# Graph product of the first layer as seven block products, with the block sums made in place by VectorE and GpSimd

## The chip, the cores and the metric

The kernel runs on one core of one Trainium2 chip. The metric is the device time of one execution in microseconds (us); lower is better. Before the change the median of three timed runs is 2531.78 us (2531.7 to 2536.01).

The engines are called as the profile calls them: PE is TensorE, DVE is VectorE, ACT is ScalarE, POOL is GpSimd, and SP is SyncE, which only issues transfers. SBUF is the on-chip memory that all of them read, PSUM the accumulators that PE writes. Each engine works through its own instructions strictly in order, and semaphores hold an instruction back until its inputs, or the buffer that it overwrites, are free.

## The reference

Two layers work on x (16 batches of 1024 rows and 256 columns, fp32) and share a 1024 x 1024 matrix `adj`. The change is in the first layer:

```python
fea = jnp.transpose(x, (0, 2, 1))                       # 256 x 1024 a batch
c_adj = jnp.mean(fea, axis=1)
diff = c_adj[:, None, :] - c_adj[:, :, None]
A = jnp.abs(jnp.abs(jax.nn.sigmoid(diff) - 0.5) - 0.5) * 2.0
Wg = adj[None, :, :] * (A + jnp.transpose(A, (0, 2, 1))) * 0.5
g = jnp.einsum('bcn,bnm->bcm', fea, Wg)                 # the graph product
q = relu(g * para)                                      # queries of 4 heads
k, v = x @ kv_w                                         # keys and values
out = softmax(q k^T * scale) v
x = layernorm(x + out)
```

For every batch the graph product multiplies 256 x 1024 by 1024 x 1024, and its result, weighted with `para` and rectified, are the queries of an attention over 1024 keys with 4 heads. The second layer (a product with a normalised `adj`, two linear maps with batch norms, a layer norm) is untouched by the change.

## The kernel before

`fast_path` does the first layer batch by batch under a manual schedule: PE, ACT, DVE and SP execute in the order in which the program is written, and POOL in an order that the framework chooses.

The attention of a batch is 32 units (2 pairs of heads x 2 halves of 512 queries x 8 blocks of 128 keys), taken two at a time: 16 bursts, u = 0 to 15. In burst u PE first makes the scores of its two units (`scores`, L952, into `ps`), ACT takes the exponential (L957, into `p`), and then `back(u-1)` multiplies the burst before with the values (`outputs`, L973, into `po`). DVE adds up the exponentials for the denominators (L981 for the first two units of a half, L983 for the others). `p` has four buffers, so an exponential needs the DVE sum of the unit four places earlier. `ps`, 128 x 1024 fp32 and two PSUM banks wide, has two buffers, and the accumulators `pg` of the graph product come from the same two. At the end of a half (u = 4, 8, 12 and 0) ACT copies `po` (L990), DVE adds to it (L991) and transposes it (L1001).

Between the bursts of batch b the written order places the preparation of batch b+1 and b+2 and the end of batch b-1:

- u = 0: values and keys of batch b+1 on PE (L902, L889), and part of its graph weights `wg`, eight tiles of 128 x 1024: ACT takes |difference| (`weights_abs`, L833) and a tanh (`weights_tanh`, L838), DVE multiplies with `adj` (`weights_adj`, L842). `side` is the list of these 24 steps, run two or three at a time.
- u = 1 and 11: `residual` of a pair of heads on POOL (L1047, L1048), after DVE reciprocals (L1041).
- u = 4: layer norm of batch b-1. `statistics_x1` is 8 pairs of DVE instructions (L620, L621), a chain of four small POOL instructions (L593, L595, L625, L626) that ends in `nm_l`, and `finish_x1` is 8 ACT instructions (L630) that need `nm_l`; then POOL issues the store of x (L1069). On PE stand here the graph product of batch b+1 for columns 0 to 127 (`graph_mm`, c = 0) and the last keys.
- u = 5: SP issues the load of x for batch b+2 and of its first half in squares of 32 x 32 (`load_squares`, L762, into `xS`, one buffer).
- u = 8: `begin` for batch b+2 on DVE (a row sum, L788, and the column means `ccol` and `ncol`, L790 and L794), a store and a broadcast load of the means by SP (L795, L797, into `crow`), the first `transpose_squares` on DVE (L813); on PE the graph product for columns 128 to 255 (c = 1) and the denominators (`normalise`, L1020).
- u = 9 to 15: first part of the weights of batch b+2; at u = 11 the second `transpose_squares`.

One half of the columns takes 16 matmuls of 128 x 128 by 128 x 512, eight in each bank of `pg`; the profile counts every fp32 matmul as two records. When all 16 are done, `queries` weights them on DVE (L861) and rectifies them on ACT (L864). Batch 0's product stands apart (`graph_first`, L874).

```python
for hs in (H0, H1):
    nc.tensor.matmul(
        s["pg"][:, hs], xt[:, n, c * P : (c + 1) * P], s["wg", n][:, hs],
        start=(n == 0), stop=(n == NCH - 1),
    )
if n == NCH - 1:
    queries(c, slice(0, N), s["pg"])
```

Of the kernel before, what the change touches and what calls it, by code (L numbers as in the profile page):

```python
# [10 lines left out]
F32 = mybir.dt.float32  # L11
I32 = mybir.dt.int32
AF = mybir.ActivationFunctionType
ALU = mybir.AluOpType
# [4 lines left out]
P = 128  # L19
# [496 lines left out]
def fast_path(  # L516
# [43 lines left out]
    def tile_s(name):  # L560
        return psum["s"].tile([P, N], F32, tag="s", name=name)
# [48 lines left out]
    def layernorm_steps(t, name):  # L610


        st = small.tile([P, NCH, 6], F32, tag="ln_st", name=f"st_{name}")
        mv = small.tile([P, NCH, 2], F32, tag="ln_mv", name=f"mv_{name}")
        rstd = small.tile([P, NCH], F32, tag="ln_rs", name=f"rs_{name}")
        nmr = small.tile([P, NCH], F32, tag="ccol", name=f"nm_{name}")

        def statistics(ns=range(NCH)):
            for n in ns:
                nc.vector.bn_stats(st[:, n, :], t[:, n, :])  # L620
                nc.vector.bn_aggr(mv[:, n, :], st[:, n, :])  # L621
            if NCH - 1 not in ns:
                return
            rsqrt(rstd, mv[:, :, 1], EPS)
            nc.gpsimd.tensor_tensor(nmr, mv[:, :, 0], rstd, ALU.mult)  # L625
            nc.gpsimd.tensor_scalar(nmr, nmr, -1.0, None, ALU.mult)  # L626

        def apply(ns=range(NCH)):
            for n in ns:
                nc.scalar.activation(  # L630
                    t[:, n, :], t[:, n, :], AF.Identity,
                    bias=nmr[:, n : n + 1], scale=rstd[:, n : n + 1],
                )

        return statistics, apply
# [68 lines left out]
    H0, H1 = slice(0, HALF), slice(HALF, N)  # L704
    C0, C1 = slice(0, P), slice(P, C)
    M0, M1 = slice(0, NCH // 2), slice(NCH // 2, NCH)
# [18 lines left out]
    graph = ExitStack()  # L725
# [7 lines left out]
    with (  # L733
# [40 lines left out]
        def prologue(b):  # L774


            s = st[b]
            xt = s["x"]
            first, steps, side = [], [], []

            def step(f, *a):
                steps.append((f, a))
# [27 lines left out]
            def transpose_squares(c):  # L810
                if c == 0:
                    s["xT"] = xTp.tile([P, CC, N], F32, tag="xT", name=f"xT_{b}")
                nc.vector.transpose(  # L813
                    s["xT"][:, c, :], s["xS", c].rearrange("p j i -> p (j i)")
                )
                if c == 0:
                    load_squares(b, 1)

            def row_of_means():

# [22 lines left out]
                    w, w, 1.0, adj_s[:, n, :], op0=ALU.subtract, op1=ALU.mult  # L843
                )

            def graph_mm(c, n):
                if n == 0:
                    s["pg"] = tile_s(f"pg_{b}_{c}")
                    if c == 0:
                        s["qT"] = qkv.tile([P, CC, N], F32, tag="qT", name=f"qT_{b}")  # L850
                for hs in (H0, H1):
                    nc.tensor.matmul(  # L852
                        s["pg"][:, hs], xt[:, n, c * P : (c + 1) * P], s["wg", n][:, hs],
                        start=(n == 0), stop=(n == NCH - 1),
                    )
                if n == NCH - 1:
                    queries(c, slice(0, N), s["pg"])

            def queries(c, hs, ps):
                q = s["qT"][:, c, hs]  # L860
                nc.vector.scalar_tensor_tensor(  # L861
                    q, ps, -scale, para_s[:, c, hs], op0=ALU.mult, op1=ALU.mult
                )
                nc.scalar.activation(q, q, AF.Relu)  # L864
# [53 lines left out]
            for i in range(4):  # L918
                step(values, i)
                step(keys, i // 2, i % 2)  # L920
            for c in range(CC if b else 0):
                for n in range(NCH):
                    step(graph_mm, c, n)
            for n in range(NCH if b == 0 else 0):
                step(graph_first, n)
            for n in range(NCH):
                side.append((weights_abs, (n,)))
                side.append((weights_tanh, (n,)))
                if n:
                    side.append((weights_adj, (n - 1,)))  # L930
            side.append((weights_adj, (NCH - 1,)))
            return first, steps, side


# [128 lines left out]
                st[b]["ln"] = layernorm_steps(st[b]["x"], f"l0_{b}")  # L1063
            st[b]["ln"][0](ns)

        def finish_x1(b, ns=range(NCH)):
            st[b]["ln"][1](ns)
            if NCH - 1 in ns:
                nc.gpsimd.dma_start(x1_d[b], st.pop(b)["x"])  # L1069

        def run(fs, k):
            for f, a in fs[:k]:
                f(*a)
            del fs[:k]
# [129 lines left out]
        with tc.manual_schedule(  # L1204
            engines={
                mybir.EngineType.PE, mybir.EngineType.Activation, mybir.EngineType.DVE,
                mybir.EngineType.SP,
            }
        ):

# [21 lines left out]
            def back(j):  # L1232

                for i in bursts[j]:
                    outputs(i)
                b, pr, qh, m = units[bursts[j][-1]]
                if m == NCH - 1 and qh == 1:
                    sums.append((normalise, (b, pr)))
                    for q in range(2):
                        full.append((residual, (b, pr, q)))  # L1240
                    if pr == PAIRS - 1:
                        late.append((statistics_x1, (b,)))
                        late.append((finish_x1, (b,)))

            last = {u: [(transpose_adjacency, (u, h)) for h in (0, 1)] for u in range(NCH)}
            for u, todo in (
# [19 lines left out]
            for j in range(len(bursts)):  # L1266
                b, u = j // PERB, j % PERB
                for i in bursts[j]:
                    scores(i)
                if u == 0:  # L1270
                    steps, side = next_steps, next_side
                    next_first, next_steps, next_side = [], [], []
                if j:
                    back(j - 1)
                if u in (5, 9, 13):
                    run(rows_of, 1)
                if u == 5 and b + 2 < B:
                    load_x(b + 2)
                    load_squares(b + 2, 0)
                    next_first, next_steps, next_side = prologue(b + 2)  # L1280
                if b == B - 1:
                    if u == 0:
                        run(sums, 1)
                        run(rows_of, 1)
                    elif u in (2, 13):
                        run(full, 2)
                    elif u == 8:
                        run(sums, 1)
                    elif u == 3:
                        late.clear()  # L1290
                elif u == 0:
                    for i in range(7):
                        if b:
                            run(steps, 1)
                            if i < 5:
                                run(side, 2)
                        if i == 1:
                            run(sums, 1)
                            run(rows_of, 1)
                elif u < 4:  # L1300
                    if u == 1:
                        run(full, 2)
                    run(side, 2 if u < 3 else 99)
                elif u == 4:
                    run(late, 1)
                    keys_last = steps[:1] if b else []
                    del steps[: len(keys_last)]
                    for n in range(NCH):
                        run(steps, 1)
                        if n == 3:  # L1310
                            run(late, 1)
                    run(keys_last, 1)
                elif u == 8:
                    run(next_first, 2)
                    run(steps, NCH)
                    run(sums, 1)
                elif u > 8:
                    if u == 11:
                        run(full, 2)
                        run(next_first, 1)  # L1320
                    run(next_side, 2 - u % 2)
                if b == B - 2:
                    run(before_last.get(u, []), 9)
                if b == B - 1:
                    run(last.get(u, []), 9)
            j = len(bursts)
# [592 lines left out]
```

## Time and profile before

| what | value |
| --- | --- |
| median of three timed runs | 2531.78 us |
| the profiled execution: time, span in the profile | 2533.89 us, 2532.1 us |
| first layer's attention, with the graph products of batches 1 to 15 | some 100 us a batch, until about 1560 us |
| ps scores L952, PE busy | 504.9 us |
| po outputs L973, PE busy | 506.6 us |
| pg graph product L852, PE busy | 420.0 us (960 records, 64 a batch) |
| pv values L902, pk keys L889, PE busy | 123.9 us, 121.9 us |
| exponentials L957, ACT busy | 495.9 us |
| sums of exponentials L983, DVE busy | 505.4 us |
| residual L1047 and L1048, POOL busy | 77.4 us and 97.5 us |

The profile is one execution, taken by the hardware profiler. Its groups give for a line and operation the output and inputs by the program's names, the number of instructions, the busy time in us, the mean of one in ns, and the idle time of the engine just before them with what ended it. A timeline row gives start and length in us, engine, line, operation, and in brackets the idle time before it and its releaser; adjacent instructions of one kind are merged into one row with a count. A row of windows gives for a stretch of time the busy time of each engine and the clock that TensorE was granted (1.00 is full speed).

### The profile page before, as it was taken

The page shows a single profiled execution, that of the slowest core. Times are in us where ns is not written, and L with a number is a line of the kernel's source. Part 1 is how long each engine was busy: PE and PEld are TensorE (multiplying, and loading weights), DVE is VectorE, ACT ScalarE, POOL GpSimd, SP SyncE. Part 2 cuts the span into 40 slices and gives each one's busy share as a digit, 9 for nine tenths or more (in the row PEclk, how much of TensorE's full clock was granted, in tenths as well). Part 3 has the DMA queues.
Part 4 walks back from the last instruction along what each step waited for, and adds up shares of the span by engine and source line. Part 5 has one row for each costly group of instructions (what it writes and reads, how often), then busy time and mean ns, then how long its engine had stood idle before and what let it go on. Part 6 is the DMA issues. An engine that isn't in the chain of part 4 may idle for free.

```text
span 2532.1 us, 32436 instructions
## 1 busy us (share of the span) xinstructions
PE 2493.3 (98%) x12646; PEld 1085.3 (43%) x12646; DVE 1606.9 (63%) x2082; ACT 1197.5 (47%) x1471; POOL 415.6 (16%) x486
## 2 busy tenths in 40 slices
PE   9999999999999999999999999999999999999997
PEld 5443443434444434434444443344444444444455
DVE  5475665765756656657657566865655566468568
ACT  6375664654755656646647555510110110144458
POOL 0011110101111111102011112431222122000026
PEclk9999999999999999999999999999999999999999
DMA  3123223132232232231322312222221222165559
GB/s 133 38 41 81 60 43 73 45 64 59 47 76 63 39 76 66 45 71 34 76 59 43 80 34 43 76 71 95 84 100 67 87 96 100 63 219 166 183 174 342
DMA packets 396978, 216.19 MB, mean 85 GB/s; under 512 B 335504, under 2 KB 368784, under 8 KB 388368
## 3 DMA queue, kind: packets, MB, share of 16 engines
q1 hardware_dynamic: 391456, 163.16, 26.0%
q0 software_dynamic: 4832, 50.34, 4.8%
q8 instruction: 101, 1.65, 0.3%
q14 instruction: 61, 0.50, 0.1%
q10 hardware_dynamic: 528, 0.52, 0.1%
HBM read 130.29 MB, written 83.69 MB: 85 GB/s over the span
## 4 chain that ended last, share of the span: by engine, by line
PE 84%; DVE 11%; DMA 2%; issue 1%; ACT 1%; SPq 1%; POOL 0%; DVEq 0%; POOLq 0%; ACTq 0%
PE ps L952 16%; PE po L973 16%; PE pg L852 15%; PE pv L902 5%; PE b_agg L1424 4%; PE pk L889 4%; PE c_agg L1424 4%; PE po L1706 3%; PE a_agg L1424 2%; PE b_h L1456 2%; PE b_o L1632 2%; PE c_h L1456 2%; PE c_o L1632 1%; PE a_h L1456 1%; PE pg L874 1%
## 5 line engine op out<-in xcount | busy, mean ns | idle before, releaser
L983 DVE TENSOR_TENSOR acc<-acc,p 128x1024 f32<-128x1024 f32 x384 | 505.4, 1316 | 146.3 <-ACT p L957 120.7
L957 ACT ACTIVATE p<-ps 128x1024 f32<-128x1024 f32 x512 | 495.9, 1021 | 155.7 <-PE ps L952 106.6
L973 PE MATMUL po<-p,v 64*64 64x512 f32 x4096 | 506.6, 589 | 1.3 <-DVE oT L991 1.3
L952 PE MATMUL ps<-qT,kT 64*64 64x512 f32 x4096 | 504.9, 593 | 2.1 <-ACT p L957 1.8
L852 PE MATMUL pg<-wg,x 128*128 128x512 f32 x960 | 420.0, 595 | 0.0
L973 PEld LDWEIGHTS po<-p,v 64*64 64x64 f32 x4096 | 172.8, 133 | 277.0 <-issue 261.5
L852 PEld LDWEIGHTS pg<-wg,x 128*128 128x128 f32 x960 | 179.9, 190 | 239.6 <-issue 215.3
L952 PEld LDWEIGHTS ps<-qT,kT 64*64 64x64 f32 x4096 | 160.2, 133 | 282.2 <-issue 217.2
L1047 POOL TENSOR_TENSOR o<-o,r_all 128x512 f32<-128x512 f32 x62 | 77.4, 1249 | 1078.5 <-DVE r_all L1041 885.3
L861 DVE SCALAR_TENSOR_TENSOR qT<-pg,para_s 128x1024 f32<-128x1024 f32 (+1 forms) x34 | 39.2, 1161 | 248.8 <-PE pg L852 246.0
L842 DVE SCALAR_TENSOR_TENSOR wg<-wg,adj_s 128x1024 f32<-128x1024 f32 x128 | 161.4, 1281 | 18.4 <-ACT wg L838 18.4
L864 ACT ACTIVATE qT<-qT 128x1024 f32<-128x1024 f32 (+1 forms) x34 | 34.2, 1009 | 264.4 <-DVE qT L861 264.4
L833 ACT ACTIVATE wg<-crow,ccol 128x1024 f32<-128x1024 f32 x128 | 146.7, 1147 | 11.4 <-DMA crow<-c 11.1
L838 ACT ACTIVATE wg<-wg 128x1024 f32<-128x1024 f32 x128 | 135.8, 1061 | 1.8
L902 PE MATMUL pv<-kvw_s,xT 128*128 128x256 f32 x512 | 123.9, 385 | 0.0
L889 PE MATMUL pk<-xT,kvw_s 128*128 128x512 f32 x256 | 121.9, 598 | 0.0
L630 ACT ACTIVATE x<-x,nm_l,rs_l 128x256 f32<-128x256 f32 x128 | 64.9, 590 | 119.9 <-POOL nm_l L626 119.9
L902 PEld LDWEIGHTS pv<-kvw_s,xT 128*128 128x128 f32 x512 | 95.0, 190 | 50.2 <-issue 28.3
L1424 PE MATMUL a_agg<-ahT,x1l 128*128 128x512 f32 x240 | 108.1, 593 | 0.7 <-ACT agg L1192 0.7
L1424 PE MATMUL b_agg<-aT,x1S 128*128 128x512 f32 x240 | 107.9, 592 | 0.0
L1048 POOL TENSOR_TENSOR x<-x,o 128x512 f32<-128x512 f32 x62 | 97.5, 1573 | 4.7
L656 ACT COPY p_agg<-a_agg 128x512 f32<-128x512 f32 x15 | 8.8, 586 | 183.3 <-PE a_agg L1424 183.3
(208 smaller groups left out, 2863.5 us busy)
## 6 DMA issues: line engine op xcount, KB each, us to landing
h<-hw POOLq DMA_DIRECT2D x16, 2048.0 KB, 6.6
hl<-h SPq DMA_DIRECT2D x32, 1024.0 KB
x<-x POOLq DMA_DIRECT2D x16, 1024.0 KB, 4.2
x1l<-x SPq DMA_DIRECT2D x16, 1024.0 KB
xf<-x SPq DMA_DIRECT2D x16, 1024.0 KB
o<-oS SPq DMA_DIRECT2D x62, 256.0 KB
o<-o SPq DMA_DIRECT2D x248, 64.0 KB
x<-in_x_dram SPq DMA_DIRECT2D x15, 1024.0 KB
```

The source lines that it names most:

```text
L833: nc.scalar.activation(w, s["crow"], AF.Abs, bias=s["ccol"][:, n : n + 1])
L838: nc.scalar.activation(w, w, AF.Tanh, scale=0.5)
L842: nc.vector.scalar_tensor_tensor(w, w, 1.0, adj_s[:, n, :], op0=ALU.subtract, op1=ALU.mult)
L852: nc.tensor.matmul(s["pg"][:, hs], xt[:, n, c * P : (c + 1) * P], s["wg", n][:, hs], start=(n == 0), stop=(n == NCH - 1),)
L889: nc.tensor.matmul(ps, kvw_s[:, c, kc * P : (kc + 1) * P], s["xT"][:, c, hs], start=(c == 0), stop=(c == CC - 1),)
L902: nc.tensor.matmul(pt[:, j * C : (j + 1) * C], s["xT"][:, c, n * P : (n + 1) * P], kvw_s[:, c, C : 2 * C], start=(c == 0), stop=(c == CC - 1),
L952: nc.tensor.matmul(ps[kh * D : (kh + 1) * D, hd * HALF : (hd + 1) * HALF], kT[r, pr, ks], qT[r, pr, qh * HALF : (qh + 1) * HALF], start=Tr ...
L957: nc.scalar.activation(p, ps, AF.Exp)
L973: nc.tensor.matmul(g["po"][kh][hd * D : (hd + 1) * D, :], s["v"][r, m, h * D : (h + 1) * D], p[r, hd * HALF : (hd + 1) * HALF], start=(m = ...
L983: nc.vector.tensor_add(g["acc"], g["acc"], p)
L1424: nc.tensor.matmul(ps, left, right, start=(start and i == 0), stop=(i == NCH // 2 - 1), skip_group_check=True,)
L1456: nc.tensor.matmul(ps, left, right, start=start, stop=True, skip_group_check=True)
```

## The change

The graph products of batches 1 to 15 are made from blocks: the 256 x 1024 left side and the 1024 x 1024 weights are each cut in 2 x 2 blocks, and the four result blocks (128 x 512) come from seven products of four matmuls each instead of eight products. The sums of blocks that this takes are made in place of blocks already used:

- left sums on POOL (`left_first`, `left_third`, `left_last`: 3, 1 and 1 instructions of 128 x 512) into a tile `S` that shares the one buffer of `xS`;
- right sums over the weight tiles: 4 instructions on DVE in `right_first`, 4 on DVE in `right_second`, 8 on POOL in `right_rest`, 128 x 512 each;
- at u = 4 the products p1, p3, p2 into one `pg` tile, at u = 8 the products p6, p7, p5, p4 into a second one; in place of the two `queries` stand two ACT copies, a POOL addition, six DVE additions or multiplications from PSUM, three DVE multiplications in SBUF and four ACT rectifications, 128 x 512 each.

Around it: POOL is now in written order as well; three of the eight ACT instructions of `finish_x1` go to POOL; the loads in squares move from u = 5 and 8 to u = 9 and 12, their transposes from u = 8 and 11 to u = 12 and 15, for `xS` and `S` share a buffer; the weights of batches from 2 on follow another order, with no DVE step before u = 0 and the last at u = 3, and two `weights_abs` at u = 8 ahead of p4.

```diff
-        def apply(ns=range(NCH)):
+        def apply(ns=range(NCH), pool=()):
+            for n in pool:
+                nc.gpsimd.tensor_scalar(
+                    t[:, n, :], t[:, n, :], rstd[:, n : n + 1], nmr[:, n : n + 1],
+                    ALU.mult, ALU.add,
+                )
...
-                if c == 0:
-                    load_squares(b, 1)
...
+            A11, A12 = xt[:, M0, C0], xt[:, M1, C0]
+            A21, A22 = xt[:, M0, C1], xt[:, M1, C1]
...
+            def left_first():
+                s["S"] = xsp.tile([P, 2, NCH // 2, P], F32, tag="xS", name=f"S_{b}")
+                s2, s4 = s["S"][:, 0], s["S"][:, 1]
+                nc.gpsimd.tensor_tensor(s2, A21, A22, ALU.add)
+                nc.gpsimd.tensor_tensor(s2, s2, A11, ALU.subtract)
+                nc.gpsimd.tensor_tensor(s4, A12, s2, ALU.subtract)
...
+            def right_first():
+                for i in KC:
+                    nc.vector.tensor_tensor(lo(i, H1), lo(i, H1), lo(i, H0), ALU.subtract)
+            def right_second():
+                for i in KC:
+                    nc.vector.tensor_tensor(hi(i, H1), hi(i, H1), lo(i, H1), ALU.subtract)
+            def right_rest():
+                for i in KC:
+                    nc.gpsimd.tensor_tensor(lo(i, H0), hi(i, H1), lo(i, H0), ALU.subtract)
+                for i in KC:
+                    nc.gpsimd.tensor_tensor(hi(i, H0), hi(i, H0), hi(i, H1), ALU.subtract)
+            def product(k, ps, start):
+                S = s["S"]
+                for i in KC:
+                    left, right = {
+                        1: (xt[:, i, C0], lo(i, H0)),
+                        2: (xt[:, i + NCH // 2, C0], hi(i, H0)),
+                        3: (S[:, 1, i], hi(i, H1)),
+                        4: (xt[:, i + NCH // 2, C1], hi(i, H0)),
+                        5: (S[:, 0, i], lo(i, H1)),
+                        6: (S[:, 0, i], hi(i, H1)),
+                        7: (S[:, 1, i], lo(i, H0)),
+                    }[k]
...
+            def weigh(c, hs):
+                nc.vector.tensor_mul(q_at(c, hs), q_at(c, hs), para_s[:, c, hs])
+                rectify(c, hs)
+            def p1():
+                s["pg"] = tile_s(f"pg_{b}_0")
...
+                product(1, s["pg"][:, H0], True)
+                nc.scalar.copy(q_at(1, H0), s["pg"][:, H0])
+            def p3():
+                product(3, s["pg"][:, H1], True)
+                nc.scalar.copy(q_at(0, H1), s["pg"][:, H1])
+                nc.gpsimd.tensor_tensor(q_at(0, H1), q_at(0, H1), q_at(1, H0), ALU.add)
+                left_third()
+            def p2():
+                product(2, s["pg"][:, H0], False)
+                nc.vector.tensor_mul(q_at(0, H0), s["pg"][:, H0], para_s[:, 0, H0])
+                rectify(0, H0)
+            def p6():
+                s["pg"] = tile_s(f"pg_{b}_1")
+                product(6, s["pg"][:, H0], True)
+                nc.vector.tensor_add(q_at(0, H1), s["pg"][:, H0], q_at(0, H1))
+                left_last()
+            def p7():
+                product(7, s["pg"][:, H0], False)
+                nc.vector.tensor_add(q_at(1, H1), s["pg"][:, H0], q_at(1, H0))
+            def p5():
+                product(5, s["pg"][:, H1], True)
+                for c in range(CC):
+                    nc.vector.tensor_add(q_at(c, H1), s["pg"][:, H1], q_at(c, H1))
+                    weigh(c, H1)
+            def p4():
+                product(4, s["pg"][:, H0], False)
+                nc.vector.tensor_add(q_at(1, H0), s["pg"][:, H0], q_at(1, H0))
+                weigh(1, H0)
...
-                        late.append((finish_x1, (b,)))
+                        late.append((finish_x1, (b, range(5), range(5, NCH))))
...
+                    if u == 2:
+                        st[b + 1]["graph"]["left"]()
...
                 elif u == 4:
+                    p, right = (st[b + 1]["graph"][key] for key in ("p", "right"))
...
+                    run(late, 1)
+                    p[1]()
+                    right[0]()
+                    run(late, 1)
+                    p[3]()
+                    p[2]()
+                    right[1]()
+                    right[2]()
                     run(keys_last, 1)
                 elif u == 8:
-                    run(next_first, 2)
-                    run(steps, NCH)
+                    p = st[b + 1]["graph"]["p"]
+                    run(next_first, 1)
+                    p[6]()
                     run(sums, 1)
+                    p[7]()
+                    p[5]()
+                    run(next_side, 2)
+                    p[4]()
```

More of the change, by code (lines that the diff above doesn't have):

```diff
@@ L844, in weights_adj, with lo, hi @@
                 )
[L846 to L851, printed above, removed]
+            A11, A12 = xt[:, M0, C0], xt[:, M1, C0]
+            A21, A22 = xt[:, M0, C1], xt[:, M1, C1]
+            def lo(i, hs):
+                return s["wg", i][:, hs]
+            def hi(i, hs):
+                return s["wg", i + NCH // 2][:, hs]
@@ new lines, in prologue, with left_third @@
+            KC = range(NCH // 2)
+            def left_first():
[4 more added lines that the diff above has]
+                nc.gpsimd.tensor_tensor(s4, A12, s2, ALU.subtract)
+            def left_third():
+                nc.gpsimd.tensor_tensor(s["S"][:, 1], A11, A21, ALU.subtract)
@@ new lines, in left_last @@
+            def left_last():
+                nc.gpsimd.tensor_tensor(s["S"][:, 0], A21, A22, ALU.add)
+            def right_first():
[9 more added lines that the diff above has]
+                    nc.gpsimd.tensor_tensor(hi(i, H0), hi(i, H0), hi(i, H1), ALU.subtract)
@@ L852, in graph_mm, with q_at @@
                     nc.tensor.matmul(
-                        s["pg"][:, hs], xt[:, n, c * P : (c + 1) * P], s["wg", n][:, hs],
-                        start=(n == 0), stop=(n == NCH - 1),
-                    )
-                if n == NCH - 1:
-                    queries(c, slice(0, N), s["pg"])
+                        ps, left, right, start=(start and i == 0), stop=(i == NCH // 2 - 1),
+                        skip_group_check=True,
+                    )
+            def q_at(c, hs):
+                return s["qT"][:, c, hs]
@@ new lines, in rectify @@
+            def rectify(c, hs):
+                q = q_at(c, hs)
+                nc.scalar.activation(q, q, AF.Relu, scale=-scale)
+            def weigh(c, hs):
[3 more added lines that the diff above has]
+                s["pg"] = tile_s(f"pg_{b}_0")
+                s["qT"] = qkv.tile([P, CC, N], F32, tag="qT", name=f"qT_{b}")
+                product(1, s["pg"][:, H0], True)
+                nc.scalar.copy(q_at(1, H0), s["pg"][:, H0])
@@ L920, in prologue @@
                 step(keys, i // 2, i % 2)
-            for c in range(CC if b else 0):
-                for n in range(NCH):
-                    step(graph_mm, c, n)
             for n in range(NCH if b == 0 else 0):
                 step(graph_first, n)
[L926 to L931, printed above, removed]
+            if b < 2:
+                for n in range(NCH):
+                    side.append((weights_abs, (n,)))
+                    side.append((weights_tanh, (n,)))
+                    if n:
+                        side.append((weights_adj, (n - 1,)))
+                side.append((weights_adj, (NCH - 1,)))
+            else:
+                a, t, j = weights_abs, weights_tanh, weights_adj
+                side += [(f, (n,)) for f, n in (
+                    (a, 0), (a, 1),
+                    (t, 0), (t, 1), (a, 2), (t, 2), (a, 3), (t, 3), (a, 4),
+                    (t, 4), (j, 0), (a, 5), (j, 1), (t, 5), (j, 2), (a, 6), (j, 3),
+                    (j, 4), (j, 5),
+                    (t, 6), (a, 7), (j, 6), (t, 7), (j, 7),
+                )]
+            if b:
+                s["graph"] = dict(
+                    left=left_first, right=(right_first, right_second, right_rest),
+                    p=(None, p1, p2, p3, p4, p5, p6, p7),
+                )
             return first, steps, side
@@ L1064, in statistics_x1, with finish_x1 @@
             st[b]["ln"][0](ns)
-        def finish_x1(b, ns=range(NCH)):
-            st[b]["ln"][1](ns)
-            if NCH - 1 in ns:
+        def finish_x1(b, ns=range(NCH), pool=()):
+            st[b]["ln"][1](ns, pool)
+            if NCH - 1 in (*ns, *pool):
                 nc.gpsimd.dma_start(x1_d[b], st.pop(b)["x"])
@@ L1206, in fast_path @@
                 mybir.EngineType.PE, mybir.EngineType.Activation, mybir.EngineType.DVE,
-                mybir.EngineType.SP,
+                mybir.EngineType.SP, mybir.EngineType.Pool,
             }
@@ L1278, in fast_path @@
                     load_x(b + 2)
-                    load_squares(b + 2, 0)
                     next_first, next_steps, next_side = prologue(b + 2)
@@ L1294, in fast_path @@
                             run(steps, 1)
-                            if i < 5:
-                                run(side, 2)
+                            run(side, 2 if i < 3 else 1)
                         if i == 1:
@@ L1302, in fast_path @@
                         run(full, 2)
-                    run(side, 2 if u < 3 else 99)
+                    if u == 2:
+                        st[b + 1]["graph"]["left"]()
+                    run(side, 1 if u == 1 else 2 if u == 2 else 99)
                 elif u == 4:
-                    run(late, 1)
+                    p, right = (st[b + 1]["graph"][key] for key in ("p", "right"))
                     keys_last = steps[:1] if b else []
                     del steps[: len(keys_last)]
[L1308 to L1311, printed above, removed]
+                    run(late, 1)
[6 more added lines that the diff above has]
+                    right[2]()
                     run(keys_last, 1)
                 elif u == 8:
-                    run(next_first, 2)
-                    run(steps, NCH)
+                    p = st[b + 1]["graph"]["p"]
+                    run(next_first, 1)
+                    p[6]()
                     run(sums, 1)
+                    p[7]()
+                    p[5]()
+                    run(next_side, 2)
+                    p[4]()
                 elif u > 8:
+                    if u == 9 and b + 2 < B:
+                        load_squares(b + 2, 0)
                     if u == 11:
                         run(full, 2)
+                    if u == 12:
                         run(next_first, 1)
-                    run(next_side, 2 - u % 2)
+                        if b + 2 < B:
+                            load_squares(b + 2, 1)
+                    if u == 15:
+                        run(next_first, 1)
+                    run(next_side, 1)
                 if b == B - 2:
```

## The prediction

> **What bounds the kernel now.** I read the engines' shares, then the chain of work that ended last, then one batch in order of time.
>
> ```profile
> PE 2493.3 (98%) x12646; PEld 1085.3 (43%) x12646; DVE 1606.9 (63%) x2082; ACT 1197.5 (47%) x1471; POOL 415.6 (16%) x486
> PE 84%; DVE 11%; DMA 2%; issue 1%; ACT 1%; SPq 1%; POOL 0%; DVEq 0%; POOLq 0%; ACTq 0%
> ```
>
> PE is busy all the time and is the chain. The other engines have slack, but all wait for each other in order, so the place matters. The timeline of one batch:
>
> ```profile
> 987.88 14.00 PE L852 MATMUL pg<-wg,x 128*128 128x512 f32 x32
> 988.00 0.59 ACT L990 COPY oT<-po 128x512 f32<-128x512 f32 x1 [0.62 <-PE po L973]
> 994.37 0.24 POOL L593 TENSOR_SCALAR rs_l<-mv_l 128x8 f32<-128x8 f32 x1 [15.07 <-DVE mv_l L621]
> 994.69 1.67 POOL L595 TENSOR_TENSOR rs_l<-rs_l,mhalf 128x8 f32<-128x8 f32 x1
> 997.01 4.04 ACT L630 ACTIVATE x<-x,nm_l,rs_l 128x256 f32<-128x256 f32 x8 [8.43 <-POOL nm_l L626]
> 1001.72 1.88 PE L889 MATMUL pk<-xT,kvw_s 128*128 128x512 f32 x4
> ```
>
> The first graph product runs without a gap from 987.88 to the keys at 1001.72: 13.84 us for 16 matmuls, 0.865 each. Beside it ACT idles 8.43 us for the layer norm's chain on DVE and POOL, then works 4 us: nobody waits for it there.
>
> ```profile
> 1017.54 0.59 ACT L990 COPY oT<-po 128x512 f32<-128x512 f32 x1 [0.62 <-PE po L973]
> 1018.16 0.69 DVE L991 TENSOR_TENSOR oT<-po,oT 128x512 f32<-128x512 f32 x1 [3.00 <-ACT oT L990]
> 1018.89 0.71 DVE L1001 STREAM_TRANSPOSE oS<-oT 128x512 f32<-128x512 f32 x1
> 1019.52 2.24 DVE L788 TENSOR_REDUCE csum<-x 128x8 f32<-128x2048 f32 x1
> 1021.88 0.16 DVE L794 TENSOR_SCALAR ncol<-csum 128x8 f32<-128x8 f32 x1
> 1036.98 1.15 ACT L833 ACTIVATE wg<-crow,ccol 128x1024 f32<-128x1024 f32 x1 [0.89 <-DMA crow<-c]
> ```
>
> At u = 8 DVE has 4.5 us of work (1017.54 to 1022.04) behind the last outputs, again hidden by 14 us of matmuls; and the first weight of the next batch starts 14.9 us after `ncol`, on its broadcast.
>
> ```profile
> 1076.12 1.04 POOL L1047 TENSOR_TENSOR o<-o,r_all 128x512 f32<-128x512 f32 x1
> 1077.25 2.13 POOL L1048 TENSOR_TENSOR x<-x,o 128x512 f32<-128x512 f32 x1
> 1076.28 4.18 DVE L983 TENSOR_TENSOR acc<-acc,p 128x1024 f32<-128x1024 f32 x2 [2.52 <-ACT p L957]
> 1082.66 5.20 DVE L983 TENSOR_TENSOR acc<-acc,p 128x1024 f32<-128x1024 f32 x4
> ```
>
> Beside POOL two sums take 4.18 us; alone four take 5.20 (1.3 each). DVE instructions with two SBUF inputs and POOL's take turns: each POOL one between two sums costs DVE some 0.8 to 0.9 us.
>
> **What the change removes.** 28 matmuls of 128x512 instead of 32: 4 x 0.865 = 3.46 us a batch, 15 batches, 51.9 us, all on PE's path. Its instruction list as built has 28, so the work does go away.
>
> **What it adds on PE's path.** In the built program PE's waits go by the whole `pg` tile, not by its banks:
> - p3 (bank H1) waits for ACT's copy of p1 (bank H0): 0.59 + 0.1 = 0.7 us.
> - p2 (H0) waits for ACT's copy of p3 (H1). Ahead of that copy on ACT stand five layer-norm instructions, which wait for POOL's `nm_l`. So the idle ACT time seen above moves into PE's queue; behind p2 stand the keys and all later scores. At best: `nm_l` 9.05 us after the product's start (997.01 - 987.95), five applications 2.55, copy 0.6: p2 at 12.3, where PE is ready at 3.46 + 0.7 + 3.46 = 7.6. That is 4.6 us.
> - p7 waits for DVE's addition of p6, which stands behind the 4.5 us of the rows above: 4.5 + 0.7 + 0.1 after the last outputs, against 3.46 (p6) + 1.0 (denominators): 0.85 us.
> - p5 waits for the addition of p7: 0.8. p4 waits for the second addition of p5, with a multiplication before it: 3 x 0.69 + 0.1 = 2.2 us.
>
> The floor is 0.7 + 4.6 + 0.85 + 0.8 + 2.2 = 9.15 - 3.46, so **+5.7 us a batch**.
>
> **What DVE and POOL add to it.** POOL's two-input 128x512 instruction takes 1.27 us alone (x<-x,o, 1074.89 in the same timeline), DVE's 0.69.
> - `left_first` (3) follows the four of `residual` directly on POOL, both beside DVE's sums of u = 1 to 3. From 1076.4 DVE has six sums (7.4), two weight steps (2.4), and seven POOL turns at 0.87 (6.1): L991 at 1092.3, where it now starts at 1088.70. The statistics are 3.6 us late, and so is `nm_l`. `right_first` (4 x 0.69 = 2.8) then meets the four small POOL instructions: 0 to 2.3 more. p2 starts between 12.3 (all in holes) and 18.3; I take 17.2, for the turns are a direct reading and only the 2.3 is open. p2's wait is then 9.6 us.
> - After p2 DVE has, alone, its multiplication 0.7, `right_second` 2.8, seven sums 8.6, the 4.5 and p6's addition 0.7: 17.3. POOL's eight of `right_rest` take turns: 0 to 8 x 0.87 = 7.0. PE gets from p2's end to p7 in 1.7 (keys) + 4 x 3.44 (bursts) + 3.46 + 1.0 = 19.9. p7 waits 0.85 to 4.4; I take 3.5, near the turns' row.
> - The three POOL applications (0.25, the small L626, to 1.27 each) run while ACT does its five: nothing, in either bound.
>
> So the batch is at -3.46 + 0.7 + 9.6 + 3.5 + 0.8 + 2.2 = **+13.3 us** (5.7 to 15.3).
>
> **The clock.** Attention has no PE gap now. Where there is one:
>
> ```profile
> 2244.68 1.10 PE L1632 MATMUL b_o<-o,w2S 128*128 128x512 f32 x2 [2.41 <-issue]
> 2241.00:2245.00 4.00, 1.59 (x4) 0.49 (x4) 3.86 (x6) 0.59 (x1) 0.00 (x0) 1.00 0.79 262
> 2245.00:2249.00 4.00, 3.74 (x6) 1.42 (x5) 3.90 (x7) 0.00 (x0) 0.00 (x0) 0.59 0.00 0
> 2441.02 1.76 PE L1787 MATMUL pf<-ident,o 128*128 128x128 f32 x7 [2.98 <-ACT o L1763]
> 2441.00:2448.00 7.00, 6.98 (x33) 6.74 (x34) 4.53 (x13) 7.00 (x7) 0.00 (x0) 0.56 0.14 59
> ```
>
> (The rows of windows end in clock, DMA share, GB/s.) After 2.41 us idle the clock was 0.59 for the next 4 us, so 4 x 0.41 = 1.6 us lost; after 2.98 us it was 0.56 for 7 us, 3.1 us lost. p2's wait is longer than either, p7's about as long. Price a batch: 0 (the lag elsewhere hides it) to 3.1 + 1.6 = 4.7; I take 1.7, one short loss, since slower matmuls behind p2 only partly meet a DVE that is late itself.
>
> [...]
>
> **What is hidden.** The broadcast: `ncol` to p6's addition 0.7, then p7, p5, p4, a burst and the waits bring PE to u = 10 at 17.6 us after `ncol`; ACT has the weights' input at 14.5, two steps 2.2, rectification 0.6, exponential 1.0: 18.3. It costs 0.7 at most, but 3.5 if p5's and p4's waits were not there. SP: the squares' load is issued when p5 frees `S`, ahead of its transpose by 3.5 + 10.3 us, the second by 10.3; today's transpose at 1043.87 comes 10.7 us after its first issue at 1033.19 without waiting. Cost 0 to 1. The store of x comes some 15 us later, its next load at about 23, the row sum at 40: nothing. The weight steps that leave u = 9 to 15 give at most 0.6 us back (that stretch runs 28.2 us for 27.5). These I take as zero together.
>
> **Sum.** Fourteen products run beside a layer norm: 14 x (13.3 + 1.7) = 210. Batch 1's has none: 0.7 + 0.7 + 0.85 + 0.8 + 2.2 - 3.46 = 1.8. The profiled execution took 2533.89 (span 2532.1): 2533.9 + 212 = 2746, about 2744 from the median of 2531.78. I say **2745**.
>
> **Rivals.**
> 1. The POOL work falls into DVE's holes and only the floor remains, with one clock loss: 14 x (5.7 + 1.7) + 2 = 106: 2638. For it: POOL is busy 16%, DVE 63%. Against: the turns at 1076 to 1081 are just where `left_first` goes.
> 2. All turns and clock losses count: 14 x (15.3 + 4.7) + 2 = 282: 2815. Against: losses overlap with a DVE that is late anyway.
> 3. Faster: the copies are done when PE asks, because ACT and DVE run ahead of PE. Place: p2 and p4. Price: each wait falls to 0.1, p7's 0.85 stays: 15 x (3.46 - 1.25) = 33: 2500. It decides from the point where the waits of a batch add up to under 3.46 us; three of them (0.7, 0.8, 2.2) contain ACT or DVE work that cannot start before PE ends, and already make 3.7.
> 4. No change: waits and saving cancel (2530 to 2535).
>
> **Chances.** Forecast 0.66, rival 1 0.16, rival 2 0.12, rival 3 0.03, rival 4 0.03. A difference under 0.2% counts as none, about what a measurement of this kernel can tell. Faster 0.03, same 0.03, slower 0.94. The range takes in the floor and the upper bound: 2620 to 2820.
>
> **What would show it.** PE idle of 7 to 11 us before p2, released by ACT's copy of p3, and that copy just behind L630's kind; 2 us before p4, 0.8 before p5, 1 to 4 before p7, each behind DVE; clock well under 1.00 after p2's gap; DVE's L991 at u = 4 some 3 us later beside POOL. No gap before p2 would prove the main step wrong; a gap of 5 would speak for rival 1.

## The result, and the profile after

The changed kernel takes **2777.88 us** (median of four runs, 2775.04 to 2778.39) beside 2531.74 us for the kernel before on the same chip: a ratio of 1.0965, interval 1.0946 to 1.0984. The forecast was 2745, range 2620 to 2820.

The page after, its shares of the engines and the chain:

```profile
PE 2508.5 (90%) x12526; PEld 1051.1 (38%) x12526; DVE 1914.2 (69%) x2307; ACT 1206.6 (43%) x1489; POOL 879.5 (32%) x738
PE 59%; DVE 30%; issue 6%; ACT 3%; POOL 2%; DMA 1%; SPq 0%; DVEq 0%; POOLq 0%
```

PE has 120 records fewer (60 matmuls) and yet is busy 15 us longer, in a span 244.5 us longer; 30% of the chain is now DVE's, 11% before. The timeline of PE in one batch; the bracket holds the idle time before a row and its releaser:

```profile
1129.77 3.70 PE L899 MATMUL pg<-wg,x 128*128 128x512 f32 x8
1134.19 3.67 PE L899 MATMUL pg<-wg,S 128*128 128x512 f32 x8 [0.72 <-issue]
1146.39 6.23 PE L899 MATMUL pg<-wg,x 128*128 128x512 f32 x8 [8.53 <-ACT qT L923]
...
1177.13 3.67 PE L899 MATMUL pg<-wg,S 128*128 128x512 f32 x8 [3.42 <-DVE qT L935]
1181.68 3.67 PE L899 MATMUL pg<-wg,S 128*128 128x512 f32 x8 [0.88 <-DVE qT L940]
1187.46 3.70 PE L899 MATMUL pg<-wg,x 128*128 128x512 f32 x8 [2.11 <-DVE qT L945]
```

These are p1, p3, p2, p7, p5 and p4. Where the kernel before ran 13.84 us without a gap, p2 now stands idle for 8.5 us and then takes 6.23 us instead of 3.7, most of it at half the clock (granted 0.50 from 1141.2 to 1151.5). The gaps of the batch add up to 15.7 us. Over the whole span the waits of PE read (total, times, longest):

```profile
PE pg L899 <- ACT qT L923: 120.2, 15, 8.5
PE pg L899 <- DVE qT L935: 48.9, 15, 3.4
```

With 31.6 us before p4, 13.1 before p5 and 10.1 before p3 that is 224 us. What holds p2 is on ACT, and what delays p7 on DVE and POOL (timelines of the same batch, one engine each):

```profile
1143.31 2.56 ACT L635 ACTIVATE x<-x,nm_l,rs_l 128x256 f32<-128x256 f32 x5 [9.21 <-POOL nm_l L626]
1145.78 0.56 ACT L923 COPY qT<-pg 128x512 f32<-128x512 f32 x1
```

```profile
1152.73 0.69 DVE L929 TENSOR_TENSOR qT<-pg,para_s 128x512 f32<-128x512 f32 x1 [10.40 <-PE pg L899]
...
1160.30 12.30 DVE L1089 TENSOR_TENSOR acc<-acc,p 128x1024 f32<-128x1024 f32 x6
```

```profile
1154.10 7.22 POOL L883 TENSOR_TENSOR wg<-wg,wg 128x512 f32<-128x512 f32 x4 [4.52 <-DVE wg L879]
1161.29 8.90 POOL L885 TENSOR_TENSOR wg<-wg 128x512 f32<-128x512 f32 x4
```

ACT idles 9.2 us for the layer norm's `nm_l`, applies it five times, and only then copies p3. The sums of exponentials beside `right_rest` take 2.05 us each, alone 1.22; POOL's sums 1.8 to 2.2, alone 1.25.

**The balance.** PE's idle time rose from 38.8 to 268.1 us (+229.3). Its busy time rose by 15.2 although 51.9 us of matmuls went, so what is left became 67.1 us longer: 229.3 + 67.1 - 51.9 = 244.5, the difference of the two spans. TensorE stood at half clock for 183 us, before for 22. PE was busy for 98 of the 183 and for 9 of the 22 us; at the granted clock of 0.50 half of that busy time is lost (where a stretch of 3.4 us falls on p7, it takes 5.37 us instead of 3.67), so by this estimate the clock itself makes 44 of the 67.1 us. The other 23 us came at full clock. An estimate for most of them: a product beside a wait takes 3.67 to 3.70 us, where in the kernel before 3.46 us brought PE four matmuls further, and 75 waits at some 0.22 us are 16 us.

### The profile page after: what moved, and what is told of

It is laid out like the page before. It is cut to its first block, busy times and chain, and to the rows that moved or that the text cites. A ratio compares the mean times of both kernels' runs of the same rounds, so it can differ in the third digit from the quotient of the medians.

```text
span 2776.6 us, 32838 instructions
## 1 busy us (share of the span) xinstructions
PE 2508.5 (90%) x12526; PEld 1051.1 (38%) x12526; DVE 1914.2 (69%) x2307; ACT 1206.6 (43%) x1489; POOL 879.5 (32%) x738
## 4 chain that ended last, share of the span: by engine, by line
PE 59%; DVE 30%; issue 6%; ACT 3%; POOL 2%; DMA 1%; SPq 0%; DVEq 0%; POOLq 0%
DVE acc L1089 10%; PE pg L899 10%; PE ps L1058 8%; PE po L1079 8%; PE pv L996 4%; PE b_agg L1546 4%; PE c_agg L1546 4%; PE pk L983 3%; PE po L1828 3%; DVE wg L879 2%; PE a_agg L1546 2%; PE b_h L1578 2%; PE b_o L1754 2%; PE c_h L1578 1%; DVE wg L845 1%
## 5 line engine op out<-in xcount | busy, mean ns | idle before, releaser
L1089 DVE TENSOR_TENSOR acc<-acc,p 128x1024 f32<-128x1024 f32 x384 | 626.3, 1631 | 54.1 <-ACT p L1063 24.5
L899 PE MATMUL pg<-wg,x 128*128 128x512 f32 x360 | 204.9, 722 | 151.9 <-ACT qT L923 120.2
L899 PE MATMUL pg<-wg,S 128*128 128x512 f32 x480 | 227.4, 618 | 72.9 <-DVE qT L935 48.9
L899 PEld LDWEIGHTS pg<-wg,x 128*128 128x128 f32 x360 | 79.6, 232 | 276.0 <-ACT qT L923 132.6
L909 ACT ACTIVATE qT<-qT 128x512 f32<-128x512 f32 x60 | 37.7, 629 | 321.4 <-DVE qT L912 220.8
L899 PEld LDWEIGHTS pg<-wg,S 128*128 128x128 f32 x480 | 88.7, 195 | 212.6 <-issue 195.0
L836 ACT ACTIVATE wg<-crow,ccol 128x1024 f32<-128x1024 f32 x128 | 145.2, 1145 | 23.3 <-DMA crow<-c 22.7
L885 POOL TENSOR_TENSOR wg<-wg 128x512 f32<-128x512 f32 x60 | 133.4, 2253 | 0.0
L697 POOL TENSOR_TENSOR x1S<-x1l 128x512 f32<-128x512 f32 x15 | 19.5, 1298 | 353.0 <-PE c_agg L1546 349.1
L883 POOL TENSOR_TENSOR wg<-wg,wg 128x512 f32<-128x512 f32 x60 | 108.3, 1834 | 62.2 <-DVE wg L879 62.2
L1154 POOL TENSOR_TENSOR x<-x,o 128x512 f32<-128x512 f32 x62 | 118.6, 1913 | 4.9
```

The source lines that it names most:

```text
L836: nc.scalar.activation(w, s["crow"], AF.Abs, bias=s["ccol"][:, n : n + 1])
L885: nc.gpsimd.tensor_tensor(hi(i, H0), hi(i, H0), hi(i, H1), ALU.subtract)
L899: nc.tensor.matmul(ps, left, right, start=(start and i == 0), stop=(i == NCH // 2 - 1), skip_group_check=True,)
L1089: nc.vector.tensor_add(g["acc"], g["acc"], p)
```

## The experiments

The kernel before ran at 2531.7, 2539.2, 2545.2 and 2531.1 us in the four sets in which the runs were timed, so kernels are compared by their ratio to it. 0.01 of the ratio is 25.3 us, 1.7 us a batch. Between two sets a ratio can be off by some 0.004, as e8 to e10 show. The changed kernel stands at 1.0965.

**Own accumulators for p3 and p5 (e1).**

```diff
-                product(3, s["pg"][:, H1], True)
-                nc.scalar.copy(q_at(0, H1), s["pg"][:, H1])
+                ps = tile_t(f"pg3_{b}")
+                product(3, ps, True)
+                nc.scalar.copy(q_at(0, H1), ps)
...
-                product(5, s["pg"][:, H1], True)
+                ps = tile_t(f"pg5_{b}")
+                product(5, ps, True)
                 for c in range(CC):
-                    nc.vector.tensor_add(q_at(c, H1), s["pg"][:, H1], q_at(c, H1))
+                    nc.vector.tensor_add(q_at(c, H1), ps, q_at(c, H1))
```

> Products p3 and p5 get accumulators of their own, one PSUM bank each, in place of the second half of pg; no instruction is added or taken away. Theory (waits by the whole tile put ACT and DVE into PE's queue): of a batch's gaps the 0.7 us before p3, 8.5 before p2, 0.9 before p5 and 2.1 before p4 go, 12.2 us, but DVE's own chain of a batch is then what p7 waits for (its gap grows from 3.4 to about 8.7) and the broadcast of the column means shows with about 3.7: net some 8 us a batch less, 15 batches, 2670 (2640 to 2710). Rival (gaps simply add up): 12.2 and some 2.6 of slow clock a batch vanish, 2778 - 15 x 14 = about 2571. Second rival (the tile is not what is waited for): 2778, p2 still waits 8.5.

Measured: 2753.62 us, ratio 1.0844 (1.0826 to 1.0862), 31 us better, where all three theories said 0 or over 60. The gaps before p3, p2, p5 and p4 are gone as the theory had it, so PE did wait for the tile; p7's gap, which the theory let grow to 8.7 us, fell to 1.2. The time was lost again elsewhere: PE waits 172 us for exponentials (4.7 in the changed kernel), and those for DVE, and PE is busy for 156 us at half clock (98 in the changed kernel). That wait of PE, one DVE row, and the POOL rows beside it:

```profile
PE ps L1060 <- ACT p L1065: 172.4, 46, 6.0
```

```profile
1018.91 13.32 DVE L1091 TENSOR_TENSOR acc<-acc,p 128x1024 f32<-128x1024 f32 x1 [1.99 <-ACT p L1065]
```

```profile
1018.86 1.28 POOL L925 TENSOR_TENSOR qT<-qT 128x512 f32<-128x512 f32 x1
1020.09 1.27 POOL L868 TENSOR_TENSOR S<-x 128x512 f32<-128x512 f32 x1
1021.31 4.94 POOL L883 TENSOR_TENSOR wg<-wg,wg 128x512 f32<-128x512 f32 x4
1026.22 4.92 POOL L885 TENSOR_TENSOR wg<-wg 128x512 f32<-128x512 f32 x4
```

One sum of 1.22 us takes 13.32 us. It starts 0.05 us behind the first of ten POOL sums, these run back to back at the 1.25 us that they take alone, and it ends 1.1 us after the last. No turns are taken here: DVE is shut out for the whole run, and PE idles 5.8 us for the next exponential. This occurs in 14 batches, 13.31 to 13.35 us each; the changed kernel has no sum over 2.3 us. A new theory was needed for it, and e7, e9 and e12 test it.

**The layer norm behind p2 (e2).**

```diff
                     right[0]()
-                    run(late, 1)
                     p[3]()
                     p[2]()
+                    run(late, 1)
```

> ACT's layer norm of the batch before (five applications, which wait for nm_l) is written behind p2 instead of ahead of p3, so the copy of p3 no longer stands behind it on ACT. Theory (p2 waits because of the queue on ACT): p2's gap falls from 8.5 to 0.7 us or less; DVE, which gains nothing from it, then makes p7 wait about 7 instead of 3.4: 2778 - 14 x (8 - 3.6 + 1.5 to 2.6 of clock), about 2663 to 2690. Rival (gaps add up): 14 x (8 + 2.6) less, about 2630. Second rival (what p2 waits for is not the queue on ACT): 2778.

Measured: 2654.72 us, ratio 1.0460 (1.0435 to 1.0485), 128 us better. Two waits of PE:

```profile
PE pg L899 <- DVE qT L935: 53.9, 14, 4.9
...
PE pg L899 <- ACT qT L923: 10.1, 15, 0.7
```

p2's wait falls from 120.2 to 10.1 us, so the queue on ACT made it. p7's grows by 5 us in all and not by 3.6 a batch: here the rival, gaps that add up, is right. DVE did not run ahead of p2: it idled 10.4 us for p2's result (L929, in the DVE rows of the changed kernel), so its whole chain up to p7 moves with p2. The gain of 128 us lies between the theory's (88 to 115) and the rival's (148). What the rival lacks is the clock: the slow stretch has moved to p7, which takes 5.2 to 6.4 us in 12 of 15 batches (in 4 in the changed kernel), and PE is still busy for 67 us at half clock: by half of the difference to 98, some 16 us came back, where the rival has 36.

**The gap filled with spare matmuls (e3).**

```diff
             def p2():
+                warm = tile_t(f"warm_{b}")
+                for i in range(8):
+                    nc.tensor.matmul(
+                        warm, xt[:, i % 4, C0], hi(i % 4, H0), start=True, stop=True,
+                    )
```

> Eight spare matmuls (8 x 0.865 = 6.9 us) into an accumulator that nobody reads stand between p3 and p2, in the time in which PE waits; the rest is unchanged. Theory (the gap lowers TensorE's clock, and that costs time of its own): PE is busy in the gap, p2 takes 3.7 us instead of 6.2, 14 batches x 2.5 = 35 us less, about 2743, although work is added; the granted clock rises from 0.967. Rival (slow matmuls meet a DVE that is late anyway, so the clock costs nothing): p7's gap grows by as much, 2778. Second rival: the spare matmuls end after the copy and delay p2, over 2778.

Measured: 2760.89 us, ratio 1.0878 (1.0860 to 1.0897): 22 us better with 104 us of matmuls more. PE in one batch:

```profile
1017.53 7.03 PE L930 MATMUL warm<-wg,x 128*128 128x512 f32 x16
1026.26 3.70 PE L899 MATMUL pg<-wg,x 128*128 128x512 f32 x8 [1.70 <-ACT qT L923]
...
1054.45 5.37 PE L899 MATMUL pg<-wg,S 128*128 128x512 f32 x8 [3.42 <-DVE qT L940]
```

p2 is back at 3.70 us, so the clock cost time of its own, and p7's gap is still 3.42: the slow clock was not hidden. But p7 now takes 5.37 us: its own gap slows it, which in the batch of the changed kernel shown above, with the same gap, it did not. Part of the slow time has only moved: p7 takes over 5 us in 9 of 15 batches, in the changed kernel in 4. PE is busy for 43 us at half clock instead of 98.

**No `right_rest` (e4).** The call `right[2]()` is deleted.

> The eight sums of right_rest on GpSimd are left out, so the products that read them use other blocks than they should; all matmuls, copies and the rest stay. Theory (GpSimd's turns lengthen VectorE's sums of exponentials between p2 and p7): the sums at u = 5 to 7 fall from 2.05 towards 1.3 us each, p7's gap from 3.4 to about 0.85, and some clock with it: 14 x 3 = 42 us less, about 2736. Rival (p7 waits for VectorE's own work, whatever GpSimd does): 2778, p7's gap stays at 3.4.

Measured: 7304.2 us as a whole, which says nothing here: with other blocks the sums of exponentials leave their range, and the kernel goes through its general path (L264, L300) as a second pass. Its first pass can be read. There p7 waits

```profile
PE pg L899 <- DVE qT L935: 16.8, 14, 1.2
```

instead of 48.9 us. The sums of exponentials between p2 and p7 take 1.23 us each instead of 1.96 on average, and from the second product on p1 follows p1 after 114.3 us instead of 116.8. So POOL's turns make 2.2 of p7's 3.4 us; DVE's own work makes 1.2.

**`left_first` at u = 0 (e5).** The call moves from u = 2 to the head of u = 0.

> The three sums of left_first on GpSimd come at u = 0 instead of u = 2; nothing is added or taken away. Theory (their turns with VectorE's sums at u = 1 to 3, 3 x 0.87 us, make the statistics late, and with them nm_l and p2): p2's gap falls from 8.5 to about 6, 14 x 2.6 = 36 us less, about 2741. Rival (the turns only move to u = 0, where VectorE has eight products with adj to make, and it is as late as before): 2778, p2's gap stays.

Measured: 2746.53 us, ratio 1.0798 (1.0780 to 1.0816), 42 us better by the ratio, 31 by the times themselves.

```profile
PE pg L899 <- ACT qT L923: 77.9, 15, 5.5
```

p2's wait lost 42.3 us, 3.0 in each of 14 batches: three turns at 1.0 us, where the theory had 0.87. Waits for exponentials grew by 5 us.

**GpSimd's order alone (e6).** The kernel before, with `mybir.EngineType.Pool` added to the engines of the manual schedule.

> The kernel before with GpSimd in written order as the only change. Theory (the loss comes from the products' waits and turns): 2532 to 2539, as before. Rival (written order alone puts GpSimd's store or its layer norm at a worse place): over 2550.

Measured: 2546.65 us beside 2545.2, ratio 1.0005 (0.9995 to 1.0014). The order as such costs nothing.

**`right_rest` on DVE, with e1 (e7).**

```diff
-            def right_rest():
-                for i in KC:
-                    nc.gpsimd.tensor_tensor(lo(i, H0), hi(i, H1), lo(i, H0), ALU.subtract)
...
+            def right_rest(part):
+                for i in range(2 * (part % 2), 2 * (part % 2) + 2):
+                    if part < 2:
+                        nc.vector.tensor_tensor(lo(i, H0), hi(i, H1), lo(i, H0), ALU.subtract)
...
+                if u in (5, 6, 7) and b < B - 1:
+                    right[2](u - 5)
...
                     right[1]()
-                    right[2]()
...
                     p[6]()
+                    right[2](3)
```

> The kernel with p3 and p5 in accumulators of their own, and besides the eight sums of right_rest on VectorE instead of GpSimd, two each at u = 5, 6, 7 and behind p6's addition. New theory (GpSimd's ten sums back to back, each 1.25 us, which is its speed alone, shut VectorE out for 13.3 us a batch, and that took the gain of the own accumulators): no sum of exponentials over 2.5 us, PE's 172 us of waiting for exponentials fall to some 50 (the broadcast of the means, and VectorE's own eight sums, 5 us), 2754 - 14 x 10 = about 2610 (2560 to 2640). Rival (VectorE has simply too much to do): its sums stay late, over 2700.

Measured: 2648.61 us, ratio 1.0405 (1.0388 to 1.0423), 111 us better than e1, with 92 us of new sums on DVE. No sum of exponentials is over 2.4 us. The gain is 33 us short of the 144, for PE still waits 96 us for exponentials: 3.4 a batch at u = 9, where ACT waits for the broadcast of the means (L836 idle 3.34 us for `crow` in one batch), and 2.9 at u = 5, where the exponentials stand behind the layer norm on ACT. The second I had left out.

**All together (e8).** e7, with the layer norm behind p2, `left_first` at u = 0, and:

```diff
-                            run(side, 2 if i < 3 else 1)
+                            run(side, 2 if i < 4 else 1)
...
-                    run(next_first, 1)
                     p[6]()
+                    run(next_first, 1)
                     right[2](3)
...
                     p[5]()
-                    run(next_side, 2)
                     p[4]()
...
-                    run(next_side, 1)
+                    run(next_side, 0 if u == 9 else 2 if u in (11, 13) else 1)
```

> All changes together: own accumulators for p3 and p5, the layer norm behind p2, left_first at u = 0, right_rest on VectorE in pairs, the row sum and column means behind p6's addition, and the first weights two bursts later. Theory (each gap has its own cause, and each is taken away): PE has no gap over 1 us in a batch, 2532 - 52 + up to 40 for small waits and the clock, 2480 to 2520. Rival (VectorE, with some 83 us of work in a batch of 96.5, in a fixed order with four buffers of exponentials, is the new bound): 2540 to 2620.

Measured: **2489.83 us, ratio 0.9787 (0.9771 to 0.9804)**, faster than both kernels. PE's chain through the products:

```profile
1055.68 3.70 PE L900 MATMUL pg<-wg,x 128*128 128x512 f32 x8
1059.22 3.60 PE L900 MATMUL pg<-wg,S 128*128 128x512 f32 x8
1062.65 3.60 PE L900 MATMUL pg<-wg,x 128*128 128x512 f32 x8
...
1086.70 7.12 PE L900 MATMUL pg<-wg,S 128*128 128x512 f32 x16
1093.65 3.60 PE L900 MATMUL pg<-wg,x 128*128 128x512 f32 x8
```

No bracket is left: p1, p3, p2, and p7, p5, p4 follow each other. From the second product on, p1 follows p1 after 97.0 us, 116.8 in the changed kernel; a batch of the kernel before takes 100.0. The gain is 0.0213 of 2531.74, 54 us, by the ratio of its own set of runs; the times as they stand give 42, and e9 and e10 43 to 45. The four matmuls make 51.9, and PE's busy time fell by 50.9 us, from 2493.3 to 2442.4. DVE is busy 75% of the span and is not the bound.

**`right_rest` on GpSimd again, in e8: in one run (e9), in pairs (e10).** e9 takes the original `right_rest`, behind p2; e10 writes `nc.gpsimd` for `nc.vector` in the eight sums.

> The kernel with all changes together (0.979 of the kernel before), but right_rest on GpSimd again, eight sums in one run behind p2. Theory of turns only (each GpSimd sum costs VectorE 0.87 us, 7.0 us a batch instead of the 5.0 of doing them itself, in a stretch where VectorE had 1 us to spare before p6's addition): 0 to 2 us a batch more, ratio 0.979 to 0.991. Theory that a run of GpSimd sums can shut VectorE out until its end: a sum of exponentials of 8 to 13 us in each batch, 5 to 8 us a batch more, ratio 1.008 to 1.03.

> The kernel with all changes together, but the eight sums of right_rest on GpSimd at the places, two by two, where that kernel has them on VectorE. Theory (a GpSimd sum costs VectorE a turn of 0.87 us where doing it costs 0.62): 2 us a batch more of VectorE's time, partly in its slack: ratio 0.979 to 0.988. Rival (handing the sums to GpSimd frees VectorE, 5 us a batch): 0.979 or less, and VectorE's busy time falls by some 75 us.

Measured: e9 2488.13 us, 0.9829 (0.9812 to 0.9845); e10 2486.46 us, 0.9822 (0.9805 to 0.9838). Both lie within what turns allow, 0.004 above e8, which was timed in another set (its absolute time, 2489.83, is the same). Neither has a sum over 2.4 us, although the run of eight is there in e9. The sums of exponentials of e10, and then of e8:

```profile
L1092 DVE TENSOR_TENSOR acc<-acc,p 128x1024 f32<-128x1024 f32 x384 | 598.3, 1558 | 45.8 <-ACT p L1066 14.8 <-DVE acc L1092 0.5
```

```profile
L1092 DVE TENSOR_TENSOR acc<-acc,p 128x1024 f32<-128x1024 f32 x384 | 546.0, 1422 | 41.7 <-ACT p L1066 15.5 <-DVE acc L1092 0.5
```

DVE does 120 sums fewer in e10 and is busy 1873.6 us instead of 1874.2. What GpSimd took over (78 us) came back as longer DVE instructions, 52 us of it in these sums: handing them over freed nothing of VectorE's time.

**One tile again, in e8 (e11).** p3 and p5 as in the change.

> The kernel with all changes together, but p3 and p5 in the second half of pg again. Theory (waits go by the whole tile): gaps of 0.7 us before p3, 0.7 before p2, 0.9 before p5 and 2.1 before p4 come back, 4.4 us x 15 = 66, none long enough for the clock: ratio 0.979 + 0.026 = 1.005. Rival (waits go by the bank, or the small gaps are hidden by what is late anyway): 0.979.

Measured: 2568.65 us, ratio 1.0152 (1.0135 to 1.0169): 0.033 above e10 of the same set, 84 us. The gaps are those of the theory, 64.9 us in all:

```profile
PE pg L900 <- DVE qT L946: 31.6, 15, 2.1
PE pg L900 <- DVE qT L941: 13.1, 15, 0.9
PE pg L900 <- ACT qT L924: 10.1, 15, 0.7
PE pg L900 <- issue: 10.1, 14, 0.7
```

Another 18 us are in PE's busy time, 2460.8 for 2442.4 in e8. Four of the 15 gaps before p4 were followed by a half-clock stretch of 3.4 us, which makes some 7 us by the busy time in such stretches; for the rest, a product behind a gap takes 3.67 to 3.70 us, where in e8 the next one starts 3.4 to 3.5 us after it. "None long enough for the clock" was wrong.

**Pairs on GpSimd, in e1 (e12).** e7 with `nc.gpsimd` for `nc.vector` in the eight sums.

> The kernel with own accumulators for p3 and p5 (ratio 1.084), with right_rest still on GpSimd but two by two at u = 5, 6, 7 and behind p6's addition instead of eight in one run. Theory (the long run shuts VectorE out): no sum of exponentials over 2.5 us, ratio near that with these sums on VectorE, 1.04 to 1.055. Rival (it is the amount of GpSimd's work, not the run): the ratio stays at 1.07 to 1.085.

Measured: 2704.26 us, ratio 1.0682 (1.0665 to 1.0700), between the two. Writing the sums in pairs did not part them:

```profile
1108.92 10.88 DVE L1092 TENSOR_TENSOR acc<-acc,p 128x1024 f32<-128x1024 f32 x1 [1.99 <-ACT p L1066]
```

Nothing in GpSimd's queue waits for a burst, so six of the eight sums still ran in one go behind `qT` and `S`, a run of eight instructions. DVE was shut out for 10.9 us, in 14 batches: two instructions fewer than in e1, 2.44 us less. In both the lock-out lasted as long as the run.

## Why the prediction was right

- **What goes.** 51.9 us of matmuls: in e8, where no product waits, PE's busy time falls by 50.9 us, and the kernel gains 54 us by the ratio of its own set of runs, 43 to 45 by that of e9 and e10.
- **p3, p5, p4.** 0.7, 0.8, 2.2 forecast; 0.72, 0.88, 2.11 measured. e11 brings just these back, at 84 us with what they do to PE's pace.
- **p2.** 9.6 forecast, 8.5 measured. Its three causes are each shown: the tile (e1 takes the gap away), the queue on ACT (e2 leaves 0.7 of it), and `left_first`'s turns (e5: 3.0, for 2.6 forecast). Some 1 us too much: `right_first` beside the four small POOL instructions cost these 0.6 us (3.27 from their start at 1140.04 to ACT's, before 2.64), where I took 1.3 of the 0 to 2.3; and PE was ready 0.5 us later than worked out.
- **p7.** 3.5 forecast, 3.42 measured, of which turns make 2.2 (e4). The one product with little more than the floor of 0.85 is the last (0.96), not batch 1's (3.42).
- **The clock is the term that was mis-sized.** I took 1.7 us a batch, "since slower matmuls behind p2 only partly meet a DVE that is late itself". By the half-clock stretches it is 44 us, 3.2 in each of 14 batches. The reason given fails: DVE waits for p2 and moves with it (e2), so the slow p2 is paid in full (e3: p7's gap is 3.42 with a fast p2 and with a slow one). The other 23 us by which PE's work became longer have no term in the forecast: a product beside a wait took 3.67 to 3.70 us at full clock as well, where 3.46 us brought PE as far before. By the balance of the spans, idle time is 229 us where the text's terms make 14 x 16.8 + 5.3 = 240, the clock 44 where they make 14 x 1.7 = 24, and the pace 23 where they have nothing: -11 + 20 + 23 are the 33 us by which the result is over the forecast, within rounding. The waits that were put too high hide a quarter of the two other errors.
- **When the clock fell.** The changed kernel's profile has 25 stretches at half clock: ten of 3.4 us, three of 6.8, eleven of 10.2, and one of 16 at the end. The other 24 began 3.0 to 4.7 us after PE had begun to idle. Each of p2's fourteen gaps of 8.5 us brought one, four of p7's fourteen of 3.42 did, four of p4's fifteen of 2.11, and two gaps of 2.4 and 3.0 in the second layer; in e11 it is again four of the fifteen of 2.11. So the length of a gap alone does not tell here whether the clock falls.
- **What was called hidden** was: PE waited 4.7 us for exponentials in all, and e6 finds nothing in the order. "3.5 if p5's and p4's waits were not there" came true in e7, at 3.4.
- **Rivals.** The result lies halfway between the forecast, 33 us under it, and rival 2 (all turns and clock losses, 2815), 37 us over it: rival 2 had the price of slow matmuls nearly right (4.7 a batch; clock and pace together are 67.1 us, 4.8 in each of 14 batches) and the waits too high. Rival 3, no waits at all, is a kernel that exists: e8. It needs several edits, for in the changed kernel the copies are never early.

Two things stay open. The forecast took turns for granted wherever DVE and POOL meet; e1 and e12 show lock-outs instead, e9 the same eight sums in turns. In e9 DVE was at its sums when the run of eight began, and in e1 and e12 it came from 2 us of idling, just behind the run's first instruction. In e7 a sum came 0.04 us behind a POOL instruction as well and was let in after that one. So what decides between turns and a lock-out is not settled. And which of e8's six edits could be left out was tried for two only: the tiles are needed (e11), `right_rest` on VectorE is not (e9).

## What to carry to other kernels

Before work is taken off the bound engine, look at what it waits for in the new order: here 3.46 us a batch were saved and 15.7 us of waits came in, all from accumulators that share a tile and from work that others had queued ahead of the copies. Give results that are read apart tiles of their own, and put work that waits long (a layer norm's tail) behind the instruction that the bound engine needs. Taking one wait away shows the next (e1, e7), so go on until the timeline of the bound engine has no bracket.

## What the runs showed of the hardware

- **Runs of GpSimd sums shut VectorE out until their end:** 13.3 us for ten in e1, 10.9 for eight in e12, though the profile shows no wait between the two. In the changed kernel they took turns: a POOL sum of 2.25 us is 1.25 as alone and 1.0 beside one DVE sum. In e9 a run of eight took turns too, with no sum of exponentials over 2.4 us.
- **Between two busy engines, a sum handed to GpSimd saved VectorE nothing:** 0.64 to 0.65 us of busy time a sum on VectorE (e8), as much again as longer DVE instructions beside GpSimd (e10).
